# A block's outputs: the centre's share added by TensorE in layer one, maximum and moments spread over two blocks in layer two

## The chip, the cores and the metric

The kernel runs on one core of a Trainium2 chip. The core has five engines with a queue of instructions each: TensorE (PE in the profile, with its weight loads as PEld), VectorE (DVE), ScalarE (ACT), GpSimd (POOL) and SyncE (SP), which here only issues DMA transfers. SBUF is the working memory with 128 partitions. PSUM is the memory that TensorE writes its results to, in banks of 512 float32 values per partition. The metric is device time in microseconds (us); lower is better.

## The reference

The model is one block of three parts, each added to `x` (16 batches, 32 channels, 512 positions): a graph attention over neighbours, a state-space scan, and a small feed-forward part. The change touches the first one only. Its inputs are coordinates of 512 nodes in each of 16 batches. Four space-filling curves (Morton and Hilbert, each with two axis orders) give four orders of the nodes. Then, twice (layer one and layer two):

```python
neigh = gather(feats, inds)                  # k = 10 neighbours of a node along a curve, for 4 curves
gf = concatenate([broadcast(center), neigh - center], axis=-1)
x16 = stack(...)[..., perm].reshape(B*N, k, total).astype(float16)   # total = 2 * C * 4 = 256
scores = einsum('bihd,bjhd->bhij', qh, qh) / sqrt(32)                # 8 heads of 32, 10 x 10 each
out = einsum('bhij,bjhd->bihd', softmax(scores), qh)
fused = out @ W_lin.T + b_lin                                        # 64 values per node and neighbour
h = einsum('oc,bnkc->bonk', W_conv, fused)                           # 32 channels in layer one, 64 in two
h = lrelu(instance_norm(h, (2, 3)))          # mean and variance over nodes and neighbours
feats_next = h.max(axis=-1)                  # greatest over the 10 neighbours
```

Normalisation and leaky ReLU are increasing functions, so the greatest value over the neighbours may be taken before them. From each block of `h` two things are then needed: the greatest of every 10 values, and the running moments (count, mean, spread) of all values.

## The kernel before

A chunk of four batches fills the 128 partitions (4 batches x 32 channels), so there are four chunks. A chunk in a layer is a stage; `order` lists the eight stages as (chunk, layer) with layers counted from 0: (0,0), (1,0), (0,1), (1,1), (2,0), (3,0), (2,1), (3,1). The text numbers them 1 to 8. Stages 1, 2, 5, 6 are layer one and stages 3, 4, 7, 8 layer two. A stage has 43 blocks of 12 nodes (the last has 8), so there are 344 blocks.

The loop at L993 is a software pipeline written out by hand: round `it` does a different step of several blocks, and every engine executes its instructions in the order in which the round writes them.

- `scores` (L812, TensorE) multiplies the neighbour differences `DD` with themselves into the bank `s`; `greatest` (L821, DVE) takes the maximum over each row of `s` with its sign turned, `c`; a round later `expo` adds `c` to `s` by TensorE (L829) and ACT takes the exponential (L834).
- `sums` (L841) and `shares` (L847 on DVE, L849 on POOL) normalise it; `turn` (L855, DVE) transposes it two rounds later.
- `mapped` (L874, TensorE, 48 matmuls, copied by ACT at L879) multiplies the differences with the folded weights. `outputs` (L893, TensorE, lag 3) multiplies attention and mapped values into the bank `h`.
- `reduce` (lag 4) takes `h` when it is full. The bank `h` holds four blocks of layer one (one tile of 480 values per partition) or two blocks of layer two (two tiles of 240). There is one such bank (`bufs=1`). DVE adds the centre's share `hc` to it and writes the sum to SBUF (L908, `hs`), then takes the maxima from `hs` (L912) and the moments (L914, one instruction for each tile).
- `hc` is that part of `h` which comes from the centre and the bias alone: one value per node and channel, the same for its 10 neighbours. It is made once per stage, by a matmul at L655 and ACT at L656.
- Beside this, `steps` does a piece of the next stage's preparation (`prep`: casts, 0/1 matrices `oh` at L723 on DVE, their matmuls at L689) or of the last stage's end (`end`, normalisation). `rank_step` compares sorting keys (L538 on TensorE, L539 on ACT), twice a round at first, then once, until 256 comparisons are done.

DVE's order in a round is thus: `turn`, `reduce` (one round in four in layer one, in two in layer two), `greatest`, `sums`, `steps`, `shares`. TensorE's is: `expo`, `scores`, comparison, `mapped`, `steps`, comparison, `outputs`. SP carries the transfers of `DX` (the differences rearranged), of the keys, and of the preparation; POOL has `shares` and the differences (L770).

Of the kernel before, what the change touches and what calls it, by code (L numbers as in the profile page):

```python
# [8 lines left out]
F32 = mybir.dt.float32  # L9
# [4 lines left out]
ALU = mybir.AluOpType  # L14
AX = mybir.AxisListType
# [3 lines left out]
P = 128  # L19
B = 16  # L20
C = 32
D = 512
NBG = 4
M = 4
K = 10
NG = 12
NGRP = -(-D // NG)
NB = 3
QB = NB * K
# [23 lines left out]
def kernel(ctx: ExitStack, tc: tile.TileContext, I, out):  # L53
# [64 lines left out]
    with ExitStack() as cx:  # L118
        graph_part(nc, tc, cx, I, dram, id32, ones, xt, U, layernorm_steps, rstd_steps, scan_input)
# [256 lines left out]
def graph_part(nc, tc, cx, I, dram, id32, ones, xt, F0, layernorm_steps, rstd_steps, scan_input):  # L376
# [10 lines left out]
    start = ExitStack()  # L387
# [14 lines left out]
    for L, co in ((1, 32), (2, 64)):  # L402
        for n, shape in (("wlA", [64, P]), ("wlC", [64, P]), ("wcT", [64, co]), ("bl", [64, 1])):
            t = wp.tile(shape, F32, name=f"{n}{L}")
            nc.sync.dma_start(out=t, in_=I[f"{n}{L}"])
            loaded[n, L] = t
    for dst, v, at in ((own, -1.0, (0, 4)), (others, 1.0, (2, 7))):
        t = kp.tile([M * B, D], BF16, name=f"sign{at[0]}")
# [12 lines left out]
    layers = []  # L421
# [127 lines left out]
    def rank_step(tile_of):  # L549

        n = ranked[0]
        if n == 4 * M * B:
            return
        ranked[0] += 1
        if n < FIRST:
            half, k = divmod(n, HALF)
            b, c, m = half % 4, k // 2, 2 * (half // 4) + k % 2
        else:
            b, k = divmod(n, 4 * M)
            c, m = divmod(k, M)  # L560
        if n == 0:
            load_keys(0, (0, 1))
        compare(tile_of(n), b, c, m)
        if n < FIRST:
            if k == 1 and half != 3 and half < 7:
                load_keys((half + 1) % 4, (0, 1) if half < 3 else (2, 3))
        elif k == 4 and b + 1 < B:
            load_keys(b + 1, range(M))
# [39 lines left out]
    sm = cx.enter_context(tc.tile_pool(name="gsm", bufs=3))  # L608
# [174 lines left out]
    live = {}  # L783
    state = {}

    def begin(at):
        g, layer = order[at]
        L, co, npair, WA, WC, HB = layers[layer]
        key = keys[at]
        per = 4 // npair  # L790
        nst = -(-NGRP // per)
        mxo = wk.tile([P, npair, D], F32, tag="mxo", name=f"mxo{key}")
        stats = wk.tile([P, npair, nst, 6], F32, tag="stats", name=f"stats{key}")
        state[at] = key, co, npair, WA, made[key][2], per, mxo, stats
# [87 lines left out]
    def outputs(at, gi):  # L882
        key, co, npair, WA, hc, per = state[at][:6]
        us, e = live.pop(("us", at, gi)), live.pop(("e2", at, gi))
        slot = gi % per
        if slot == 0:
            live["h", at] = ps_1.tile([P, npair, per * NQ], F32, tag="h", name=f"h{at}_{gi}")
        h = live["h", at]
        for j in range(NJ):
            for b in range(4):  # L890
                pr, r = divmod(b * co, P)
                q0 = slot * NQ + j * QB
                nc.tensor.matmul(  # L893
                    h[r:r + co, pr, q0:q0 + QB], lhsT=us[:, j, b * co:(b + 1) * co],
                    rhs=e[:, 4 * j + b, :QB], start=True, stop=True,
                )
        if slot == per - 1 or gi == NGRP - 1:
            live["full", at, gi] = h

    def reduce(at, gi):  # L900
        key, co, npair, WA, hc, per, mxo, stats = state[at]
        h = live.pop(("full", at, gi), None)
        if h is None:
            return
        f0 = (gi - gi % per) * NG
        nn = min((gi + 1) * NG, D) - f0
        hs = sm.tile([P, npair, per * NG, K], F32, tag="hs", name=f"hs{at}_{gi}", bufs=1)
        nc.vector.tensor_tensor(  # L908
            hs[:, :, :nn], h[:, :, :nn * K].rearrange("p r (n j) -> p r n j", j=K),
            hc[:, :, f0:f0 + nn].unsqueeze(3).to_broadcast([P, npair, nn, K]), ALU.add,  # L910
        )
        nc.vector.tensor_reduce(mxo[:, :, f0:f0 + nn], hs[:, :, :nn], AX.X, ALU.max)  # L912
        for pr in range(npair):
            nc.vector.bn_stats(stats[:, pr, gi // per], hs[:, pr, :nn].rearrange("p n j -> p (n j)"))  # L914
        if gi == NGRP - 1:
            tails.append(end(at))

    def end(at):

        g, layer = order[at]  # L920
        key, co, npair, WA, hc, per, mxo, stats = state.pop(at)
        res = []
        for pr in range(npair):
            mv = sm.tile([P, 2], F32, tag="mv", name=f"mv{key}_{pr}")
            nc.vector.bn_aggr(mv, stats[:, pr].rearrange("p k s -> p (k s)"))
            r = sm.tile([P, 1], F32, tag="hr", name=f"hr{key}_{pr}")
            yield from rstd_steps(sm, r, mv[:, 1:2], 1, f"h{key}_{pr}")
            dst = F1[g] if layer == 0 else wk.tile([P, D], F32, tag=f"F2_{pr}", name=f"F2_{key}_{pr}", bufs=1)
            yield from lrelu_norm(dst, mxo[:, pr], mv[:, 0:1], r, f"{key}_{pr}")
            res.append(dst)  # L930
        if layer == 1:
            yield from finish(g, res)

    def lrelu_norm(dst, src, mean, r, key):
        t = wk.tile([P, D], F32, tag="lr", name=f"lr{key}", bufs=1)
        nc.vector.tensor_scalar(t, src, mean, r, ALU.subtract, ALU.mult)
        yield
        nc.vector.scalar_tensor_tensor(dst, t, 0.2, t, ALU.mult, ALU.max)
        yield

    def junk(q):
        return wk.tile([P, D], F32, tag="h3", name=f"usq{q}", bufs=1)

    def finish(g, F2):
        p3 = ps_1.tile([P, D], F32, tag="misc", bufs=2, name=f"p3_{g}")
        for j, f in enumerate((F0[:, g], F1[g], *F2)):
            nc.tensor.matmul(p3, lhsT=W3[:, j], rhs=f, start=(j == 0), stop=(j == 3))
        h3 = wk.tile([P, D], F32, tag="h3", name=f"h3_{g}", bufs=1)
        nc.scalar.copy(h3, p3)
        yield  # L950
        n3 = wk.tile([P, D], F32, tag="n3", name=f"n3_{g}", bufs=1)
        yield from layernorm_steps(sm, n3, h3, f"f{g}")
        yield
        nc.vector.scalar_tensor_tensor(n3, n3, 0.2, n3, ALU.mult, ALU.max)
        nc.vector.tensor_tensor(xt[:, g], xt[:, g], n3, ALU.add)

    made = {}
    order = [(0, 0), (1, 0), (0, 1), (1, 1), (2, 0), (3, 0), (2, 1), (3, 1)]
# [13 lines left out]
    def steps(at, gi):  # L972


        if tails:
            if next(tails[0], tails) is tails:
                tails.pop(0)
            return
        if at + 1 >= len(order):
            return  # L980
        if at + 1 not in ahead:
            if at > 0 and gi < 4:
                return
            ahead[at + 1] = [prep(*order[at + 1]), PREP]
        a = ahead[at + 1]
        for _ in range(2 if a[1] > NGRP - LEAD - 1 - gi else 1):
            if next(a[0], None) is False:
                break
            a[1] -= 1

    ahead = {}
    blocks = [(at, gi) for at in range(len(order)) for gi in range(NGRP)]
    for it in range(len(blocks) + 4):  # L993

        def do(step, lag):
            if 0 <= it - lag < len(blocks):
                step(*blocks[it - lag])

        at, gi = blocks[it] if it < len(blocks) else (len(order), 0)
        if gi == 0 and it < len(blocks):  # L1000
            begin(at)
        do(expo, 1)
        do(turn, 3)
        do(scores, 0)
        do(reduce, 4)
        rank_step(later_tile)
        do(greatest, 0)
        do(mapped, 0)
        do(sums, 1)
        if at + 1 == len(order) and gi == 4:  # L1010
            tails.extend(scan_input(sm, junk(q), q) for q in range(NBG - 1))
        steps(at, gi)
        do(shares, 1)
        if ranked[0] < 8 * 4 * M:
            rank_step(later_tile)
        do(outputs, 3)
        if it + LEAD < len(blocks):
            to, g2 = blocks[it + LEAD]
            if g2 == 0:
                for _ in ahead[to][0]:  # L1020
                    pass
            differences(to, g2)
# [384 lines left out]
```

## Time and profile before

| | |
|---|---|
| median of 3 runs | 2433.89 us (2430.68 to 2434.2) |
| profiled execution | 2429.63 us, span from first to last instruction 2427.9 us |
| TensorE busy | 2137.0 us, 88% of the span; weight loads 1249.5 us |
| DVE busy | 1739.6 us, 72% |
| ACT busy | 1099.8 us, 45% |
| POOL busy | 831.7 us, 34% |
| granted TensorE clock | 0.969 of full, mean |
| L908 (addition) | 132 instructions, 81.8 us, 620 ns each |
| L912 (maxima) | 132 instructions, 84.2 us, 638 ns each |
| L914 (moments) | 220 instructions, 89.1 us, 438 ns each |

Busy time is the union of an engine's instructions. TensorE's ends are modelled and some of its records can be missing, so its idle time is to be read with care. In the waits, "A <- B: total, times, longest" says that A's engine stood idle until B ended. In the groups, the time after the second bar is idle time of the engine just before them. In a timeline, columns are start, length (both in us), engine, line, operation, and in brackets idle time before it and what ended it. An instruction's start on DVE may come a little before the one before it ends, so prices of a queue are read from start to start.

### The profile page before, as it was taken

The numbers are of one execution on the slowest core, as the hardware profiler recorded it, in microseconds if no ns is written. First come the engines' busy times: TensorE is split into PE (matmuls) and PEld (weight loads), VectorE is DVE, ScalarE is ACT, GpSimd is POOL, SyncE is SP. The second block draws the span as 40 slices with busy tenths as digits, with TensorE's granted clock in tenths as the row PEclk, the third lists the DMA queues.
The fourth block names the chain that finished last, engine by engine and source line by source line (L and its number), as shares of the span: only waits on it lengthen the run. The fifth ranks groups of instructions, "written<-read, shape, count | busy, mean of one in ns | idle before, by whom it ended". The sixth has DMA issues, their size and how long they took to land. (4 is left out here: it accounts for less than half of the span.)

```text
span 2427.9 us, 88565 instructions
## 1 busy us (share of the span) xinstructions
PE 2137.0 (88%) x39024; PEld 1249.5 (51%) x39146; DVE 1739.6 (72%) x3718; ACT 1099.8 (45%) x2023; POOL 831.7 (34%) x897
## 2 busy tenths in 40 slices
PE   5598687999898777789999789999999999999979
PEld 2254455677666455557767544444444444444422
DVE  8498798888898899989999866553553626446643
ACT  6686556667554334345555323333332423333331
POOL 2165556445445465664645300020211202021200
PEclk9899899999999989999999889999999999999989
DMA  1323232231132231422311312203112131210000
GB/s 48 79 54 76 49 77 59 50 72 40 36 71 51 51 83 42 95 49 55 68 38 35 96 48 73 76 26 100 52 57 67 38 87 40 81 54 22 27 36 18
DMA packets 121625, 137.99 MB, mean 57 GB/s; under 512 B 18398, under 2 KB 79506, under 8 KB 121154
## 3 DMA queue, kind: packets, MB, share of 16 engines
q1 hardware_dynamic: 121240, 132.32, 22.1%
q8 instruction: 307, 5.03, 0.9%
q14 instruction: 78, 0.64, 0.1%
HBM read 77.02 MB, written 12.85 MB: 37 GB/s over the span
## 5 line engine op out<-in xcount | busy, mean ns | idle before, releaser
L849 POOL TENSOR_TENSOR EN<-e,rz 128x480 f32<-128x480 f32 x344 | 342.9, 997 | 562.7 <-DVE rz L847 417.8
L874 PE MATMUL u<-WA,DD 128*32 128x128 bf16 (+1 forms) x16512 | 421.9, 251 | 53.7 <-issue 36.7
L874 PEld LDWEIGHTS <-DD 128*32 128x32 f16 x16512 | 341.5, 99 | 71.8 <-issue 67.9
L879 ACT COPY us<-u 128x512 f32<-128x512 f32 x516 | 302.1, 587 | 152.5 <-PE u L874 134.2
L834 ACT ACTIVATE e<-s,smc 128x480 f32<-128x480 f32 x344 | 227.6, 662 | 293.6 <-PE s L829 266.0
L770 POOL TENSOR_TENSOR DD<-fs,crep 128x480 f16<-128x480 f32 (+2 forms) x344 | 350.2, 1019 | 0.0
L893 PE MATMUL h<-e,us 128*32 128x30 f32 (+1 forms) x11008 | 283.7, 211 | 57.4 <-DVE e L855 27.5
L893 PEld LDWEIGHTS h<-e,us 128*32 128x32 f32 (+1 forms) x11008 | 250.9, 127 | 145.0 <-issue 46.9
L1105 DVE SCALAR_TENSOR_TENSOR cyh<-ppch,t_conv_w,cyh 128x496 f32<-128x496 f32 (+2 forms) x192 | 137.4, 716 | 221.4 <-ACT cyh L1100 217.5
L821 DVE TENSOR_REDUCE c<-s 128x16 bf16<-128x480 f32 x344 | 218.9, 636 | 72.7 <-PE s L812 70.2
L1181 POOL TENSOR_TENSOR da<-lei,dA 128x512 f32<-128x512 f32 x32 | 40.6, 1271 | 612.5 <-PE pl L1186 577.9
L1254 PE MATMUL po<-wo,gs 128*128 128x512 f32 x512 | 240.5, 605 | 10.8 <-DVE xt L1257 10.6
L1093 PE MATMUL ppch<-hT,winch 128*128 128x512 f32 x512 | 232.2, 593 | 0.0
L1093 PE MATMUL ppg<-hT,wing 128*128 128x512 f32 x512 | 231.9, 593 | 0.0
L855 DVE STREAM_TRANSPOSE e<-EN 128x512 f32<-128x512 f32 x344 | 224.3, 652 | 0.6 <-POOL EN L849 0.6
L841 DVE TENSOR_REDUCE z<-e 128x16 f32<-128x480 f32 x344 | 219.0, 637 | 0.0
L539 ACT ACTIVATE sgn<-kd 128x512 bf16<-128x512 f32 x256 | 153.1, 598 | 56.8 <-PE kd L538 28.2
L723 DVE TENSOR_SCALAR oh<-it,rank 128x512 bf16<-128x512 f16 x512 | 168.7, 389 | 8.5 <-PE pp L689 8.5
L812 PEld LDWEIGHTS <-DD 128*32 128x32 f16 x5504 | 82.1, 97 | 164.1 <-issue 127.7
L829 PE MATMUL s<-c,idb 128*128 128x480 bf16 x344 | 131.6, 383 | 36.2 <-DVE c L821 33.4
L812 PE MATMUL s<-DX,DD 128*32 128x120 f16 x5504 | 144.0, 224 | 20.3 <-DMA DX<-DD 17.0
L1093 PEld LDWEIGHTS ppch<-hT,winch 128*128 128x128 f32 x512 | 93.7, 190 | 122.7 <-issue 122.3
(323 smaller groups left out, 2748.1 us busy)
## 6 DMA issues: line engine op xcount, KB each, us to landing
DX<-DD SPq DMA_DIRECT2D x456, 90.0 KB
wo<-in_out_proj SPq DMA_DIRECT2D x64, 256.0 KB
wing<-in_in_proj SPq DMA_DIRECT2D x64, 256.0 KB
winch<-in_in_proj SPq DMA_DIRECT2D x64, 256.0 KB
crep<-dC SPq DMA_DIRECT2D x128, 64.0 KB
dS<-so SPq DMA_DIRECT2D x32, 256.0 KB
fs<-dS SPq DMA_DIRECT2D x128, 64.0 KB
wincB<-in_in_proj SPq DMA_DIRECT2D x8, 256.0 KB
```

What stands on the lines that cost most here:

```text
L770: nc.gpsimd.tensor_tensor(d[:, :, m0 - n0:n1 - n0], win, crep[:, :, m0:n1].unsqueeze(3).to_broadcast([P, 4, n1 - m0, K]), ALU.subtract,)
L812: nc.tensor.matmul(s[rh, j * 4 * QB:(j + 1) * 4 * QB].rearrange("p (b q) -> p b q", b=4), lhsT=d[:, h, c0:c0 + 32], rhs=dx[:, h, :, c0:c0 ...
L821: nc.vector.tensor_reduce(c, live["s", at, gi].rearrange("p (i q) -> p i q", q=QB), AX.X, ALU.max, negate=True)
L834: nc.scalar.activation(e, s.rearrange("p (i q) -> p i q", q=QB), AF.Exp, scale=smc)
L841: nc.vector.tensor_reduce(z, e, AX.X, ALU.add)
L849: nc.gpsimd.tensor_tensor(en[:, :, :QB], e, rz.unsqueeze(2).to_broadcast([P, NI, QB]), ALU.mult)
L855: nc.vector.transpose(e.rearrange("p i q -> p (i q)"), en.rearrange("p i q -> p (i q)"))
L874: nc.tensor.matmul(u[rh, jj], lhsT=d[:, h, c0:c0 + 32], rhs=WA[k][:, h].rearrange("p b o -> p (b o)"), start=(jj == 0 and k == 0), stop=(k ...
L879: nc.scalar.copy(us[:, j - jj:j + 1], u)
L893: nc.tensor.matmul(h[r:r + co, pr, q0:q0 + QB], lhsT=us[:, j, b * co:(b + 1) * co], rhs=e[:, 4 * j + b, :QB], start=True, stop=True,)
L1093: nc.tensor.matmul(pp, lhsT=w[:, k], rhs=hT[:, k], start=(k == 0), stop=(k == 3))
L1254: nc.tensor.matmul(po, lhsT=gs[:, i, q * P:(q + 1) * P], rhs=wo[i], start=(i == 0), stop=(i == TG - 1))
```

## The change

In layer one (`npair == 1`), the first `outputs` of a group now begins with one more matmul: the identity `id32` times `hc`, each value repeated 10 times, put into all used columns of the bank `h`. The 64 matmuls (16 in each of four blocks) of the group's `outputs` that follow add to it (`start=False`), where they overwrote before. DVE's addition L908 is gone in layer one; maxima and moments read the bank `h` itself, so the bank is in use until both have read it.

In layer two the addition stays. In the round of the addition only the moments of the first tile are taken. The maxima and the moments of the second tile are kept as a function in `live["rest", at]`, and are executed in the next round by the new step `rest`, ahead of `reduce`; after the last group of a stage at once. The loop has one more round.

```diff
         if slot == 0:
             live["h", at] = ps_1.tile([P, npair, per * NQ], F32, tag="h", name=f"h{at}_{gi}")
+            if npair == 1:
+
+                f0 = gi * NG
+                nn = min(f0 + per * NG, D) - f0
+                nc.tensor.matmul(
+                    live["h", at][:, 0, :nn * K].rearrange("p (n j) -> p n j", j=K), lhsT=id32,
+                    rhs=hc[:, 0, f0:f0 + nn].unsqueeze(2).to_broadcast([P, nn, K]), start=True, stop=False,
+                    skip_group_check=True,
+                )
...
-                    rhs=e[:, 4 * j + b, :QB], start=True, stop=True,
+                    rhs=e[:, 4 * j + b, :QB], start=npair > 1, stop=True, skip_group_check=True,
...
-        hs = sm.tile([P, npair, per * NG, K], F32, tag="hs", name=f"hs{at}_{gi}", bufs=1)
-        nc.vector.tensor_tensor(
-            hs[:, :, :nn], h[:, :, :nn * K].rearrange("p r (n j) -> p r n j", j=K),
-            hc[:, :, f0:f0 + nn].unsqueeze(3).to_broadcast([P, npair, nn, K]), ALU.add,
-        )
-        nc.vector.tensor_reduce(mxo[:, :, f0:f0 + nn], hs[:, :, :nn], AX.X, ALU.max)
-        for pr in range(npair):
-            nc.vector.bn_stats(stats[:, pr, gi // per], hs[:, pr, :nn].rearrange("p n j -> p (n j)"))
+        hs = h[:, :, :nn * K].rearrange("p r (n j) -> p r n j", j=K)
+        if layers[order[at][1]][0] == 2:
+            t = sm.tile([P, npair, per * NG, K], F32, tag="hs", name=f"hs{at}_{gi}", bufs=1)
+            nc.vector.tensor_tensor(
+                t[:, :, :nn], hs, hc[:, :, f0:f0 + nn].unsqueeze(3).to_broadcast([P, npair, nn, K]), ALU.add,
+            )
+            hs = t[:, :, :nn]
+
+        def greatest_of():
+            nc.vector.tensor_reduce(mxo[:, :, f0:f0 + nn], hs, AX.X, ALU.max)
+
+        def moments(pr):
+            nc.vector.bn_stats(stats[:, pr, gi // per], hs[:, pr].rearrange("p n j -> p (n j)"))
+
+        if npair == 1:
+            greatest_of()
+            moments(0)
+        else:
+            moments(0)
+            live["rest", at] = lambda: (greatest_of(), moments(1))
         if gi == NGRP - 1:
+            rest(at, gi)
             tails.append(end(at))
+
+    def rest(at, gi):
+        if ("rest", at) in live:
+            live.pop(("rest", at))()
...
-    for it in range(len(blocks) + 4):
+    for it in range(len(blocks) + 5):
...
+        do(rest, 5)
         do(reduce, 4)
```

## The prediction

> **What bounds the kernel now.** I read the busy time by stretches first. The graph part runs from 117 to about 1376 us as eight stages of 43 blocks; the stretches below are cut at the first exponential of each stage. Stages 1, 2, 5, 6 are layer one, stages 3, 4, 7, 8 layer two (columns: length; busy time of PE, weight loads, DVE, ACT, POOL; granted clock; DMA).
>
> ```profile
> 117.00:267.00 150.00, 123.83 (x4409) 72.86 (x4418) 122.85 (x271) 104.11 (x242) 84.32 (x93) 0.95 0.29 62
> 267.00:414.00 147.00, 112.31 (x4422) 75.47 (x4461) 129.78 (x288) 88.34 (x183) 86.24 (x95) 0.95 0.30 65
> 414.00:585.00 171.00, 158.35 (x4419) 118.96 (x4457) 146.58 (x337) 113.11 (x224) 86.57 (x96) 1.00 0.25 56
> 585.00:763.00 178.00, 164.60 (x4424) 122.48 (x4450) 153.79 (x365) 104.56 (x203) 86.23 (x95) 0.96 0.24 52
> 763.00:915.00 152.00, 114.70 (x4422) 77.00 (x4421) 138.96 (x319) 58.71 (x101) 86.16 (x96) 0.92 0.29 62
> 915.00:1056.00 141.00, 107.20 (x4415) 72.90 (x4414) 129.24 (x284) 58.97 (x97) 86.28 (x95) 0.96 0.30 65
> ```
>
> Layer two is TensorE's: 158 of 171 us and 165 of 178 us, and most of its blocks come at even steps of 3.21, 3.65 or 4.29 us with TensorE idle 0 to 0.25 us in each. Layer one differs by stage. In stages 5 and 6 DVE is busy 91 to 92% and TensorE 75 to 76%; in stage 1 the two are level (82%). There the two engines take turns at the lead, so neither total alone tells what an edit is worth. Next I read who waits for the exponent's constant, `c`: one line of the waits in each layer-one stretch, in order of time.
>
> ```profile
> PE s L829 <- DVE c L821: 1.8, 4, 0.6
> PE s L829 <- DVE c L821: 5.6, 8, 1.4
> PE s L829 <- DVE c L821: 11.5, 10, 1.4
> PE s L829 <- DVE c L821: 7.6, 10, 1.4
> ```
>
> In stages 2, 5 and 6 TensorE waits for `c` in 28 blocks, nearly always the one in four whose DVE work has the three `reduce` steps ahead of `greatest`. Stage 1 hardly has this wait: with two rank comparisons per block TensorE arrives later than `c`. The timeline of one reduce block in stage 5 shows the wait, and one in stage 1 its absence:
>
> ```profile
> 859.47 0.61 DVE L908 TENSOR_TENSOR hs<-h,hc 128x480 f32<-128x480 f32 x1
> ...
> 860.13 0.46 PE L893 MATMUL h<-e,us 128*32 128x30 f32 x32 [0.47 <-DVE hs L908]
> ...
> 861.94 0.36 PE L829 MATMUL s<-c,idb 128*128 128x480 bf16 x1 [1.35 <-DVE c L821]
> ```
>
> ```profile
> 137.93 0.46 PE L893 MATMUL h<-e,us 128*32 128x30 f32 x32
> ...
> 138.44 0.36 PE L829 MATMUL s<-c,idb 128*128 128x480 bf16 x1
> ```
>
> The groups give the prices (line, engine, shape, count | busy, mean ns | idle before):
>
> ```profile
> L908 DVE TENSOR_TENSOR hs<-h,hc 128x480 f32<-128x480 f32 x124 | 78.7, 635 | 31.3 <-PE h L893 31.2
> L912 DVE TENSOR_REDUCE mxo<-hs 128x48 f32<-128x480 f32 x124 | 81.0, 653 | 4.3
> L914 DVE BATCH_NORM_STATS2 stats<-hs 128x6 f32<-128x480 f32 x40 | 26.0, 650 | 0.0
> L821 DVE TENSOR_REDUCE c<-s 128x16 bf16<-128x480 f32 x344 | 218.9, 636 | 72.7 <-PE s L812 70.2
> L841 DVE TENSOR_REDUCE z<-e 128x16 f32<-128x480 f32 x344 | 219.0, 637 | 0.0
> L655 PE MATMUL ph<-c,WC 128*128 128x512 f32 x24 | 16.4, 769 | 15.3 <-DVE c L650 14.5 <-ACT us L879 0.7
> ```
>
> **Removed: the layer-one addition.** Four stages have 11 groups each (ten of 48 nodes and one of 32), so 44 of the 132 additions go. In the block above L908 starts at 859.47 and L912 at 860.11, 0.64 us apart, so DVE gets 44 x 0.64 = 28 us back, if DVE is what the block waits for.
>
> **Added: one seed matmul per layer-one group.** No such instruction is in the trace; the nearest row is L655, also f32 with a full 128x128 weight. Each is two records; in the timeline the work behind it starts 1.06 or 1.07 us after it in 7 of 12 cases, with the first weight load exposed, and once 0.93 us; projections of L1093, with loads hidden, follow each other at 0.43 us per record. For 480 of 512 columns that is 0.80 us (loads hidden) to 1.0 us. I take 0.9 us, nearer the first, since the identity waits for nothing and can be loaded ahead: 44 x 0.9 = 40 us of TensorE. The seed adds no DMA and nothing on POOL or ACT.
>
> **The seed waits longer for the bank.** There is one `h` bank. It was free after L908; now it is free after the maximum and the moments, 0.6 us later. Behind the waiting seed stand the group's `outputs`, the next block's L829 and its scores, and ACT's exponential waits for those. [...] The row decides otherwise: after the block above, bank free at 860.75 (859.47 + 0.58 + 0.65 + 0.05), seed to 861.65, outputs 0.4, next L829 at 862.05. Before it stood at 861.94, held by `c`. `c` is now ready at 861.25. So the wait for `c` is exchanged for the seed, at +0.1 us on TensorE and -0.64 us on DVE.
>
> **Reading the bank twice.** [...] The trace has the same reduction from both memories, L821 from the bank and L841 from SBUF: 636 and 637 ns. [...]
>
> **What the layer-one stages make of it**, group by group, from the idle time of both engines:
> - Stage 1: in 8 of 11 groups TensorE is idle 0 to 1.0 us in 12 to 13 us (one, 2.8), and DVE mostly 0.8 to 2.2. The seed lies in the open: 8 x 0.9 = 7.2, less what idle time swallows, +5.5 (ends +2, +8). Its stall of 14.5 us for the transfer into `fs` (at 236 us) stays as it is.
> - Stage 2: one comparison per block is left. Five groups have DVE full (idle under 0.2) and TensorE with 2.2 to 2.8 us idle, some of which are lost matmul records; they gain about 0.2 each. The others lose about 0.2: in the block at 304 us the next L829 goes from 307.0 to 307.5. Sum 0 (-2, +4).
> - Stages 5 and 6: twelve groups with DVE full gain. Not the whole 0.64: after the block above, scores would be ready at 866.9 and DVE at 866.8, so 0.45 on average, 12 x 0.45 = 5.4; ten groups lose 0.1. Sum -4.4 (-8, +2).
>
> **Layer two: one order exchanged for another.** The 88 additions stay; the maximum and one moment move to the next block, ahead of its `greatest`. DVE's sum over two blocks stays. In the block with the addition, `c` comes 0.57 + 0.32 = 0.9 us earlier; in the next DVE starts 0.9 us earlier and does 0.9 us more first, so `c` comes when it did, or into slack of 1.0 us or more. What can be won is TensorE's wait for `c` there: 0, 0.7, 1.5 and 5.1 us in the four stages, 7.3 us. But in stages 7 and 8, where it lies, DVE is idle only 0.1 to 0.5 us per four blocks: it is full, and the wait would return elsewhere. At the change of stages the chain of casts to L655 stands behind a reduce (TensorE waits 2.7 and 3.6 us) and could win 0.9 each. I take -2.5 (-5, 0). The bank is freed by the addition as before, the moved steps issue nothing on SP or POOL and pass no wait of another engine, and the last group of a stage is finished at once as before; the loop's one extra round has nothing else to do.
>
> **Sum.** +5.5 + 0 - 4.4 - 2.5 = -1.4 us. The profiled execution took 2429.63 us (span 2427.9 and 1.7 around it); it becomes 2428.2. The median of the runs is 2433.89, 4.3 above it; against that, **2432.5 us**.
>
> **Rivals.** *DVE leads nearly everywhere (faster).* For it: DVE's 88 to 92% in stages 2, 5, 6. Nineteen DVE-full groups at the whole 0.64 are -12, layer two's waits in part -4, stage 1 only +3: -13, 2421 us. Against: DVE idles 12 to 28 us in each of these stages.
> *TensorE leads after the seed (slower).* 44 x 0.9 = 40 us of seeds, of which the waits for `c` in layer one cover 26.5, and nothing of DVE's gain is seen: +13, 2447 us. It decides once TensorE has under 0.9 us of true idle time per group; stage 1 has that. Against: 1.9 to 4.7 us are idle in the full-DVE groups of stages 5 and 6.
> *The gains and losses cancel:* my forecast. There the change does what it says in each stage, and the total does not show it.
>
> **How the numbers follow.** About 0.2% (4.9 us) is what a measurement of this kernel can tell from no change. My case 0.5, faster rival 0.27, slower rival 0.23. My case by itself spans 2426 to 2439, so it gives 0.06 to faster and 0.02 to slower: faster 0.33, same 0.42, slower 0.25. Adding all good ends gives -13, all bad ends +14; the range reaches to about two thirds of either, 2424 to 2442.
>
> **What would show it.** L908's successor has 88 entries; layer-one maximum and moments near 640 to 660 ns from the bank; 88 seed records at 0.8 to 1.0 us per pair. The first stage 2 to 8 us longer, stages 5 and 6 shorter by 1 to 4 each, TensorE's wait for `c` in layer one nearly gone, replaced by waits of the seed for the moments. I am wrong if the seed takes over 1.2 us, if reading the bank costs DVE 60 ns or more, if stages 5 and 6 do not shorten, or if layer two moves by more than 5 us.

## The result, and the profile after

The changed kernel takes 2415.49 us (median of 6 runs, 2411.28 to 2418.40) against 2433.89 us: a ratio of 0.9924 with a 95% interval of 0.9911 to 0.9937, so 18.4 us faster. The forecast was 2432.5 us with a range of 2424 to 2442; the result lies below it, and most of the miss is in layer two. Measured twice more, beside other kernels, the ratio was 0.9928 and 0.9933.

The profiled execution took 2416.21 us (span 2414.5). Busy time by stretches, stages 1 to 6, in the columns of the prediction (length; PE, weight loads, DVE, ACT, POOL; granted clock; DMA):

```profile
114.00:268.00 154.00, 137.11 (x4445) 76.11 (x4444) 117.45 (x263) 104.97 (x242) 85.57 (x95) 0.94 0.29 62
268.00:412.00 144.00, 127.72 (x4447) 74.98 (x4445) 121.85 (x274) 88.50 (x182) 86.39 (x96) 0.99 0.30 66
412.00:586.00 174.00, 171.71 (x4490) 120.65 (x4489) 143.52 (x333) 113.12 (x224) 85.82 (x95) 0.98 0.25 55
586.00:757.00 171.00, 167.62 (x4456) 119.86 (x4452) 151.74 (x365) 104.60 (x203) 85.61 (x95) 0.99 0.25 55
757.00:910.00 153.00, 120.82 (x4449) 76.72 (x4446) 132.71 (x310) 58.82 (x101) 86.22 (x95) 0.93 0.28 60
910.00:1052.00 142.00, 113.23 (x4438) 72.20 (x4436) 122.70 (x275) 58.89 (x96) 87.22 (x97) 0.98 0.30 65
```

In layer one DVE has 5.4 to 7.9 us less to do per stage. In layer two (third and fourth line) it should have exactly what it had, since no instruction was removed; yet it is busy 143.52 instead of 146.58 us and 151.74 instead of 153.79. That is the first sign of the cause. The groups by shape (count | busy, mean ns | idle before):

```profile
L919 DVE TENSOR_TENSOR hs<-h,hc 128x480 f32<-128x480 f32 x84 | 54.0, 642 | 27.3 <-PE h L902 27.3
L925 DVE TENSOR_REDUCE mxo<-hs 128x48 f32<-128x480 f32 x84 | 51.0, 607 | 0.0
L892 PE MATMUL h<-hc,id 128*128 128x480 f32 x80 | 42.7, 617 | 13.8 <-DVE stats L928 12.8 <-DVE hs L919 0.9
L925 DVE TENSOR_REDUCE mxo<-h 128x48 f32<-128x480 f32 x40 | 25.1, 626 | 4.1 <-PE h L902 4.0
L928 DVE BATCH_NORM_STATS2 stats<-h 128x6 f32<-128x480 f32 x40 | 25.9, 648 | 0.0
L829 PE MATMUL s<-c,idb 128*128 128x480 bf16 x344 | 132.4, 385 | 5.5 <-DVE rz L847 3.2 <-DVE c L821 1.3
```

The seed (L892) is two records; from its start to the outputs behind it 0.90 to 1.00 us pass in 38 of the 40 full groups, median 0.97. Maxima and moments read from the bank cost 626 and 648 ns, no more than the 653 and 650 ns from SBUF in the kernel before. TensorE's wait for `c` (last row) is 1.3 us in all. In the kernel before it was 33.4 us:

```profile
L829 PE MATMUL s<-c,idb 128*128 128x480 bf16 x344 | 131.6, 383 | 36.2 <-DVE c L821 33.4
```

The seed now waits 12.8 us for the moments. By window, in stages 2, 5 and 6:

```profile
PE h L892 <- DVE stats L928: 2.5, 3, 1.3
PE h L892 <- DVE stats L928: 7.4, 6, 1.9
PE h L892 <- DVE stats L928: 2.8, 4, 1.0
```

### The profile page after: what moved, and what is told of

It is laid out like the page before. It is cut to its first block, busy times and chain, and to the rows that moved or that the text cites. A ratio compares the mean times of both kernels' runs of the same rounds, so it can differ in the third digit from the quotient of the medians.

```text
span 2414.5 us, 88867 instructions
## 1 busy us (share of the span) xinstructions
PE 2190.0 (91%) x39234; PEld 1248.1 (52%) x39234; DVE 1699.6 (70%) x3674; ACT 1100.1 (46%) x2023; POOL 831.6 (34%) x897
## 5 line engine op out<-in xcount | busy, mean ns | idle before, releaser
L879 ACT COPY us<-u 128x512 f32<-128x512 f32 x516 | 302.0, 587 | 149.5 <-PE u L874 131.8
L821 DVE TENSOR_REDUCE c<-s 128x16 bf16<-128x480 f32 x344 | 220.7, 642 | 107.0 <-PE s L812 104.4
L855 DVE STREAM_TRANSPOSE e<-EN 128x512 f32<-128x512 f32 x344 | 224.4, 652 | 0.0
L841 DVE TENSOR_REDUCE z<-e 128x16 f32<-128x480 f32 x344 | 219.5, 638 | 0.0
L723 DVE TENSOR_SCALAR oh<-it,rank 128x512 bf16<-128x512 f16 x512 | 158.0, 368 | 7.5 <-PE pp L689 7.5
L1120 PEld LDWEIGHTS ppg<-hT,wing 128*128 128x128 f32 x512 | 95.8, 190 | 114.0 <-issue 114.0
```

The lines of the kernel that those rows point to most:

```text
L821: nc.vector.tensor_reduce(c, live["s", at, gi].rearrange("p (i q) -> p i q", q=QB), AX.X, ALU.max, negate=True)
L841: nc.vector.tensor_reduce(z, e, AX.X, ALU.add)
L855: nc.vector.transpose(e.rearrange("p i q -> p (i q)"), en.rearrange("p i q -> p (i q)"))
L879: nc.scalar.copy(us[:, j - jj:j + 1], u)
L1120: nc.tensor.matmul(pp, lhsT=w[:, k], rhs=hT[:, k], start=(k == 0), stop=(k == 3))
```

## The experiments

Unless said otherwise an edit is to the kernel before, and the figure is the median against the kernel before measured beside it, with the ratio's interval. From here on "comparison" means an instruction of L723, by which VectorE makes a 0/1 matrix `oh`, and not the comparison of keys on TensorE (L538). "Held" counts those of L723 that take over 500 ns; the kernel before has 48 in layer one and 13 in layer two.

### Each layer alone

One kernel has layer one as changed and layer two as before, the other the reverse:

```
# l1_only: layer two keeps its order       # l2_only: no seed, addition in both layers
 else:                                      if False:                     # the seed
+    greatest_of()                          ...
+    moments(0)                             if True:                      # the addition
+    moments(1)                             (the split of layer two as changed)
```

> Layer one as in the changed kernel (seed by TensorE, no addition on DVE), layer two as before. The theory read from the two traces: layer one's four stages change by +1 to +3 us in all (seed in the open in stage 1, gain in the others), so the ratio is 0.999 to 1.002. The rival that DVE leads layer one nearly everywhere: -8 to -14 us, ratio 0.994 to 0.997. The rival that the seed leads: +8 us or more, ratio over 1.003.

> Layer one as before, layer two as in the changed kernel (maxima and second moments a round later). The theory read from the two traces: layer two carries the gain, -10 to -16 us, ratio 0.993 to 0.996, and TensorE's wait for c in the layer-two stages falls from 7 us to under 2. The forecast's own sum for layer two: -2.5 us, ratio 0.998 to 1.000.

> Layer one as changed, layer two as before, once more, beside layer two alone. If the two parts share a gain, or the first measurement was high, this run and the next one come to 17 to 20 us together; if they add up only to 26 us again, the two parts share some 8 us when both are there. This one alone: -10.5 us again if its first value stands, -4 to -7 us if it was high.

> Layer two as changed, layer one as before, once more, beside layer one alone. -15.4 us again if its first value stands; -11 to -13 us if it was high.

Layer one alone: 2425.74 against 2436.26 us (0.9956, 0.9942 to 0.9969), and again 2428.56 against 2433.30 (0.9971, 0.9957 to 0.9986): 7 to 10.5 us faster. Layer two alone: 2420.84 against 2436.26 (0.9935, 0.9922 to 0.9948), and again 2420.54 against 2433.30 (0.9944, 0.9926 to 0.9963): 13 to 15.4 us faster. So both parts gain, layer two more. By the mean ratios the parts would make 23 us together, and the whole kernel gains 16 to 18; what the two have in common in these 5 to 6 us was not found, and with intervals of some 3 us on each part it may in part be measurement.

### The addition and the seed by themselves

`l1_nocentre` drops the addition in layer one and adds no seed; it leaves the centre's share out there. `l1_seedcost` keeps the addition and seeds the bank with zeros:

```
# l1_nocentre                               # l1_seedcost
-if npair == 1:   # seed                    -rhs=hc[:, 0, f0:f0 + nn]...
+if False:                                  +rhs=nil...     # zeros
 if layer is two:  # addition               -if layer is two:  # addition
                                            +if True:
```

> Layer one without the addition on DVE and without the seed, so the centre's share is left out of layer one's values; maxima and moments read the bank; layer two as before. It shows what DVE's 28 us are worth when TensorE pays nothing. My group count (DVE full in 19 groups, 0.64 us each, and nothing elsewhere): -8 to -13 us, ratio 0.9945 to 0.997. If DVE leads everywhere: -20 to -28 us. If TensorE leads and the longer hold of the bank hurts: 0 to -4 us.

> Layer one keeps VectorE's addition as before and TensorE puts a product of zeros into the bank as well, so the 44 seed matmuls (40 us of TensorE by the forecast's 0.9 us each) come on top and nothing is taken away; layer two is as before. By the forecast the seed lies in the open in the eight groups of stage 1 and in half of it elsewhere: +5.5 us in stage 1 and +8 to +14 us in all. By the difference of the runs with and without the seed (2425.74 less 2423.55) it costs about +2 us: 0 to +4. More than +8 says that the forecast priced the seed rightly and only VectorE's part wrongly.

Without the additions: 2423.55 us (0.9951, 0.9938 to 0.9964), 12 to 13 us of the 28 that VectorE no longer works. With the seed on top and nothing taken away: 2431.72 against 2432.01 us (1.0008, 0.9996 to 1.0019), some 2 us at most 5. So the forecast's share in the open was too large. Where the forty microseconds of matmuls went is less plain: TensorE's idle time took them, or in part its clock paid for them, for the mean granted clock of these executions is 0.970 against 0.964 beside it. No run separates the two.

### Earlier greatest values without the spreading

`l2_late` issues layer two's maxima and second moments in the same round, but behind `greatest`:

```
 do(reduce, 4)
 do(greatest, 0)
+do(rest, 4)
```

> Layer one as before. In layer two the maxima and the second tile's moments stay in the same round, but stand behind greatest on DVE's queue instead of ahead of it. If the gain of layer two comes only from c being ready earlier for TensorE, this gives the same as the split over two rounds, -10 to -16 us. If it comes from spreading DVE's work over two rounds, at most half of it, 0 to -6 us, because sums, the 0/1 matrices and shares of that round come as late as before.

2431.24 against 2436.26 us (0.9986, 0.9977 to 0.9996): 3 to 5 us of layer two's 13 to 15. So the earlier `c` is worth a quarter to a third, and something in spreading the work over two rounds is worth the rest.

### What the spreading removes

The trace shows it. A round without a reduction in stage 7 of the kernel before, VectorE and then GpSimd (start, duration, engine, line, operation):

```profile
1141.92 0.65 DVE L855 STREAM_TRANSPOSE e<-EN 128x512 f32<-128x512 f32 x1
1142.50 0.62 DVE L821 TENSOR_REDUCE c<-s 128x16 bf16<-128x480 f32 x1
1143.05 0.63 DVE L841 TENSOR_REDUCE z<-e 128x16 f32<-128x480 f32 x1
1143.60 1.50 DVE L723 TENSOR_SCALAR oh<-it,rank 128x512 bf16<-128x512 f16 x4
...
1142.17 1.00 POOL L849 TENSOR_TENSOR EN<-e,rz 128x480 f32<-128x480 f32 x1 [2.77 <-DVE rz L847]
1143.13 1.03 POOL L770 TENSOR_TENSOR DD<-fs,crep 128x480 f16<-128x480 f32 x1
```

Four comparisons take 1.50 us. In the round with a reduction ahead of this one they take 1.13 us, from 1140.72. Here the first of them started while GpSimd subtracts (`DD`, 1143.13 to 1144.16) and takes 0.71 us; it ends 0.15 us after the subtraction does. The same kind of round in the changed kernel:

```profile
1132.91 0.65 DVE L855 STREAM_TRANSPOSE e<-EN 128x512 f32<-128x512 f32 x1
1133.49 0.60 DVE L925 TENSOR_REDUCE mxo<-hs 128x48 f32<-128x480 f32 x1
1134.02 0.39 DVE L928 BATCH_NORM_STATS2 stats<-hs 128x6 f32<-128x240 f32 x1
1134.33 0.64 DVE L821 TENSOR_REDUCE c<-s 128x16 bf16<-128x480 f32 x1
1134.89 0.64 DVE L841 TENSOR_REDUCE z<-e 128x16 f32<-128x480 f32 x1
1135.45 1.13 DVE L723 TENSOR_SCALAR oh<-it,rank 128x512 bf16<-128x512 f16 x4
...
1134.12 1.04 POOL L770 TENSOR_TENSOR DD<-fs,crep 128x480 f16<-128x480 f32 x1
```

The deferred maxima and moments now stand ahead, the subtraction runs beside moments and reductions, which take no longer for it (0.39 and 0.64 us here; by their rows 0.40 and 0.64), and the comparisons begin after it: four in 1.13 us. GpSimd starts its two operations when `rz` is there, so they end 2.4 us after `rz` starts; `rz`, the transposition, `c` and `z` fill only 1.84 us of VectorE, and the deferred 0.84 us bridge the gap. In stage 7 the comparisons' row goes from

```profile
L723 DVE TENSOR_SCALAR oh<-it,rank 128x512 bf16<-128x512 f16 x64 | 22.1, 402 | 0.0
```

to

```profile
L723 DVE TENSOR_SCALAR oh<-it,rank 128x512 bf16<-128x512 f16 x64 | 18.4, 346 | 0.0
```

3.7 us, and the stage, from its first exponential to the next stage's, from 159.9 to 155.9 us. Stage 8 has no comparisons, but small instructions met the subtraction there. In the kernel before:

```profile
1268.03 0.58 DVE L76 TENSOR_TENSOR rsh_s<-rsr_s 128x1 f32<-128x1 f32 x1
1268.64 0.16 DVE L77 TENSOR_TENSOR rsh_s<-rsh_s,rst_s 128x1 f32<-128x1 f32 x1
...
1267.56 1.03 POOL L770 TENSOR_TENSOR DD<-fs,crep 128x480 f16<-128x480 f32 x1
```

In the changed kernel:

```profile
1259.11 0.15 DVE L76 TENSOR_TENSOR rsh_s<-rsr_s 128x1 f32<-128x1 f32 x1
1259.29 0.16 DVE L77 TENSOR_TENSOR rsh_s<-rsh_s,rst_s 128x1 f32<-128x1 f32 x1
```

An instruction on one column takes 0.58 us instead of 0.15. In layer two of the kernel before, 13 comparisons lose 4.8 us in this way and some ten other instructions (L76, L641, L938, L954) 4.3 us, some 9 us together; in the changed kernel one of them is left (an L76, 0.4 us). With the 3 to 5 us of the earlier `c` that is 12 to 14 us of layer two's 13 to 15; the sum is near, and each part has some 2 to 3 us of doubt.

One rival is the granted clock, which also differs between the kernels (see the last section). It can be set aside where a stage has the same clock in both: stage 7 takes 159.9 us before and 155.9 to 156.2 us in three profiles of the changed kernel, all at 0.98; stage 8 takes 151.7 and, in the profile with full clock, 148.4 us, both at 1.00. So these two stages gain 3 to 4 us each without it.

Not every instruction of VectorE that starts while GpSimd works is held. In the rounds above L723 is (0.71 us) and L76 is (0.58 us); L821, which starts inside the subtraction at 1134.33, is not (0.64 us). Over the whole trace of the kernel before, 65 comparisons start while an instruction of GpSimd has over 0.25 us to go, with a median of 709 ns against 345 for those beside none; 31 transpositions (L855) that start so take 653 ns, like the others, and 41 moments of 240 columns (L914) 400 ns against 395. What in the hardware sets the one kind apart from the other, no run here shows.

### Taking the subtraction away

GpSimd's subtraction is cut to the first node of each block outside stage 1; the other nodes' differences are left out. The same with layer one, and with layer two, as changed:

```
 m0 = max(first, half)
+if at > 0 and first > 0:
+    n1 = m0 + 1
```

> The kernel before, with GpSimd's subtraction of each block (1.03 us) cut to its first node from the third stage's blocks on and in the second stage's as well, except in a tile's first block; the other nodes' differences are left out, and nothing else is changed. VectorE's one-hot comparisons (L723) that start while that subtraction runs take 0.7 us instead of 0.34, 54 of them in stages 2 to 7, 20.3 us in all beyond 0.345 us each. If VectorE is held there by GpSimd, these long ones go to nearly none, and the time falls: by the 5.5 us of stages 3, 4 and 7 if layer one has the room to hide its part, by 10 to 14 us if layer one's part counts at the rate that its additions counted (12.7 us for 28). If the long ones have another cause, they stay and the time moves by less than 2 us.

> Layer one as changed, layer two as before, and GpSimd's subtraction cut to one node as in the run of the kernel before with the short subtraction (-27.3 us; the other nodes' differences are left out). If layer one gains by VectorE's additions alone, it gains as much on top of that run as on top of the kernel before: -34 to -39 us against the kernel before. If part of its gain is that its comparisons meet GpSimd less often (17.3 us before, 13.0 us with layer one changed), that part is gone: -31 to -34 us.

> Layer two as changed, layer one as before, and GpSimd's subtraction cut to one node (the other nodes' differences are left out). If layer two's gain is that its comparisons no longer meet GpSimd's subtraction (5.5 us of waiting before, 0.4 after, and some 1.5 us more in the other instructions that met it), at least 5 us of its 15 are already in the run with the short subtraction: -33 to -38 us. If the gain has nothing to do with GpSimd, all 15 us come on top of it: -40 to -44 us. If it is all GpSimd's, nothing comes on top: -26 to -30 us.

The kernel before with the short subtraction: 2404.76 against 2432.01 us (0.9884, 0.9868 to 0.9901), held comparisons 6 and 0. That is 27 us, at least twice what was expected, and near the waiting that is gone: 20 us of the comparisons and 4 us of the other instructions in layer two. On top of it the changes are worth nothing that can be measured. Layer two: 2404.36 against 2433.30 (0.9884, 0.9859 to 0.9909), as expected if its gain is all GpSimd's. Layer one: 2411.76 against 2433.30 (0.9906, 0.9888 to 0.9924). That is some 5 us slower than without the change, where 4 to 12 us faster had been expected; across two batches, with about 6 us of doubt, the slowdown is not shown, but the expected gain is not there. The run has the seed and the missing addition together, so it does not say which of them fails to pay.

These runs take most of a microsecond of GpSimd's work from each block besides the meeting, so they don't settle the cause alone, nor that all of the 27 us is VectorE's waiting.

### The meeting itself

Both kernels keep all work and add the same 54 instructions to VectorE, a reduction that nobody reads, in rounds in which the kernel before has a held comparison (54 of its 61). One puts it ahead of that comparison, the other behind:

```
+if count[0] in PADS:      # the held ones; or each of them + 1
+    nc.vector.tensor_reduce(pad1, id32[:, :118]...[P, 3, 118], AX.X, ALU.max)
+count[0] += 1
 nc.vector.tensor_scalar(oh, it2, rank..., None, ALU.is_equal)
```

> The kernel before with 54 more instructions on VectorE, each a reduction of 354 elements that nobody reads (about 0.43 us from its start to the next one's; 23 us in all), each directly ahead of one of the comparisons that take 0.7 us in the kernel before. If those comparisons are held until GpSimd's subtraction ends, the added instruction runs inside that time, the comparison behind it takes 0.34 us, and the time stays within 0 to +4 us. If they are slow for a reason of their own, the added work counts as VectorE's work does: +10 to +20 us.

> The same 54 instructions in the same rounds, but each one behind the comparison that is held and ahead of the next comparison. The comparison is held as before and the added work comes on top: +10 to +20 us at the rate of the additions in layer one (12.7 us for 28 us) up to nearly the whole of 23 us. If VectorE's time doesn't decide these rounds, or if the hold is of no account, it stands within 3 us of the run with the instructions ahead.

Ahead: 2430.18 against 2431.03 us (0.9994, 0.9982 to 1.0006). Behind: 2447.49 against 2431.03 (1.0070, 1.0052 to 1.0088). The same 23 us of added work cost nothing in the one place and 16 us in the other. The timeline of a round with the instruction ahead (held comparisons left: 4 and 0):

```profile
877.61 0.63 DVE L847 TENSOR_REDUCE z<-e 128x16 f32<-128x480 f32 x1
878.16 0.50 DVE L727 TENSOR_REDUCE pad<-id 128x3 f32<-128x354 f32 x1
878.59 1.13 DVE L729 TENSOR_SCALAR oh<-it,rank 128x512 bf16<-128x512 f16 x4
...
877.69 1.03 POOL L776 TENSOR_TENSOR DD<-fs,crep 128x480 f16<-128x480 f32 x1
```

and of the same round with it behind (48 and 15):

```profile
877.67 0.62 DVE L847 TENSOR_REDUCE z<-e 128x16 f32<-128x480 f32 x1
878.22 0.71 DVE L729 TENSOR_SCALAR oh<-it,rank 128x512 bf16<-128x512 f16 x1
878.85 0.51 DVE L727 TENSOR_REDUCE pad<-id 128x3 f32<-128x354 f32 x1
...
877.75 1.03 POOL L776 TENSOR_TENSOR DD<-fs,crep 128x480 f16<-128x480 f32 x1
```

The reduction that starts inside the subtraction runs at once (0.50 us); the comparison that starts there takes 0.71 us and ends 0.15 us after the subtraction does. So the meeting is what makes these comparisons long, and the time that VectorE loses by it counts: GpSimd's load is the same in both runs.

### Two ways around it, and the order once more

`after_ddsplit` issues the subtraction of the changed kernel as two halves. `split_both` has no seed and keeps VectorE's addition in layer one, but spreads it: addition, maxima, moments in three rounds.

```
# after_ddsplit                             # split_both, from l2_only
+mid = (m0 + n1) // 2                       if npair == 1:
+for ma, mb in ((m0, mid), (mid, n1)):      -    greatest_of(); moments(0)
     nc.gpsimd.tensor_tensor(...)           +    live["rest", at] = [greatest_of, lambda: moments(0)]
```

> The changed kernel once more, beside the other runs of this batch. If layer one alone (-10.5 us) and layer two alone (-15.4 us) add up, it stands 24 to 28 us under the kernel before. If the two get part of their gain from the same place, it stands 16 to 21 us under it, as in its own measurement (-18.4 us).

> The changed kernel with GpSimd's subtraction of a block issued as two of half the nodes, about 0.55 us each. If a comparison that VectorE starts during it is held until the instruction of GpSimd ends and not until the queue is empty, the 34 long comparisons that are left in layer one become shorter (12.2 us beyond 0.345 us each falls to 4 or less) and the time falls by 2 to 6 us against the changed kernel of this batch. If GpSimd's second half gets in ahead of the waiting comparison, they stay as long or longer, and the time is the same or up to 3 us more.

> Layer two as changed; layer one keeps VectorE's addition, has no seed, and spreads its reduction over three rounds: the addition in one, the maxima in the next, the moments in the third. VectorE has 28 us more to do than in the changed kernel, but three of four rounds in layer one, and not one of four, have 0.55 us of other work ahead of the comparisons. If the meeting with GpSimd decides, the long comparisons of layer one fall from 48 (32 in the changed kernel) to 16 or fewer, and the time is 2402 to 2412 us, below the changed kernel. If VectorE's total work decides, it is that of layer two alone or worse: 2418 to 2424 us.

> The changed kernel beside these two: 16 to 19 us under the kernel before, as in the two measurements before (ratios 0.9924 and 0.9928).

The halves: 2412.14 us beside 2414.43 for the changed kernel in the same batch (ratios to before 0.9915, 0.9900 to 0.9930, and 0.9928, 0.9914 to 0.9941), no difference; 41 comparisons are held in layer one, no fewer. In the trace all 41 start when the first half has ended (0 to 0.19 us before) and the second has begun, and each ends 0.15 us after the second half does. So they meet the second half alone, and the run does not show which would go first if a comparison stood waiting between the two.

`split_both`: 2409.12 us beside 2416.51 for the changed kernel (0.9906, 0.9892 to 0.9921, and 0.9933, 0.9920 to 0.9946). It is 7 us faster than the changed kernel though VectorE adds in both layers as before; its held comparisons are 13 in layer one (29 to 34 in the changed kernel) and none in layer two. It is the fastest complete version here.

`after_cfirst` was to defer layer two's maxima to the next round and put them behind `greatest` there:

```
-do(rest, 5)
 do(reduce, 4)
 do(greatest, 0)
+do(rest, 5)
```

> The changed kernel with the deferred maxima and second moments issued behind the next scores' greatest values instead of ahead of them; VectorE's work in each round is the same and the comparisons still stand behind it. If TensorE still waits for the greatest values in layer two, the time falls by 2 to 5 us against the changed kernel (2414 to 2416 us). If its wait for them is gone, as the trace of the changed kernel says (1.3 us in all), it stays within 2 us.

> The changed kernel with the maxima and second moments of layer two really deferred to the next round, and there issued behind the greatest values of the next scores. No comparison of layer two is held in either order, since the work ahead of the comparisons is the same. TensorE's wait for the greatest values is 1.3 us in all in layer two, so the time stays within 2 us of the changed kernel; if the earlier greatest values are worth something that the waits do not show, it falls by 3 to 5 us.

`after_cfirst` did not do so. Behind the reduction the call finds that round's own maxima and runs them at once, which makes it layer one as changed with `l2_late`, not what its expectation says. As that it fits: 2421.14 against 2431.03 us (0.9962, 0.9950 to 0.9975), 13 comparisons held in layer two again, and half of the changed kernel's gain gone. `after_cfirst2` remembers the block and defers in fact: 2423.80 us beside 2416.51 (0.9954, 0.9941 to 0.9966), none held in layer two, and still 7 us slower where 2 at most had been expected. Its profiled execution has a span of 2417.8 us against 2416.6, too near to find those 7 us in; they stay unexplained.

## Why the prediction was wrong

**Layer two, the step that failed.** "DVE's sum over two blocks stays", and then: in stages 7 and 8 "it is full, and the wait would return elsewhere": -2.5 us, at most -5. Measured: -13 to -15. DVE's instructions stayed the same; their durations did not. Part of what its row counts as busy was waiting for GpSimd, some 9 us in layer two, and the new order put other work into that time. The prediction shows what would have told this: its price rows hold a mean, and the comparisons of L723, which have a median of 345 ns and a maximum of 721 over the whole kernel, do not appear in it.

**Layer two, the chain of hand-offs and the earlier `c`.** Right in kind: TensorE's wait for `c` fell from 33.4 to 1.3 us in all. `l2_late` prices the earlier `c` at 3 to 5 us, where the forecast had -2.5 for all of layer two.

**Seed.** 0.9 us was near (0.97). What was wrong is where it lies: stage 1 was to be 5.5 us longer, and all 44 seeds on top of the old kernel cost about 2 us. From first exponential to first exponential, stage 1 takes 148.6 and 149.5 us in the two profiles of layer one alone and 152.7, 148.3 and 152.8 us in three of the changed kernel, against 149.5: no steady 5.5.

**The bank held longer.** Right: reading the bank costs nothing more (626 and 648 ns against 653 and 650), and the seed waits 12.8 us in all for the moments, where 0.6 us in each of the 44 groups would be 26 us.

**Layer one as a whole.** Forecast +1.1; measured -7 to -10.5. "28 us, if DVE is what the block waits for" was the right condition; 12.7 of the 28 came (`l1_nocentre`), not 5.4 on twelve groups. The step that failed is thus the count of groups in which VectorE leads. Why it leads in more of them than the idle times said is shown in part only: the held comparisons lose 17.2 us in layer one before and 12.6 and 11.8 us in the two profiles of layer one alone, and with the subtraction short the gain is gone. The rest stays open.

**The rivals.** "DVE leads nearly everywhere", at 2421 us, had the right sign and came nearest, but its layer two (-4) was sized by the same step. What was held against it, that DVE idles 12 to 28 us in each of these stages, reads the rows too high: in stages 2, 5 and 6 the length less the busy time is 17, 13 and 12 us, and 27 belongs to stage 1.

## What to carry to other kernels

Before calling an engine full, ask its rows for the spread of a duration, not the mean: an instruction whose maximum is twice its median may be waiting inside its own busy time, and a change of order elsewhere can then win that back. In this kernel the ones to look at were VectorE's instructions that start inside GpSimd's subtraction: the comparisons L723 (a median of 709 ns against 345), the cast L641 (850 against 426) and the one-column L76 (580 against 150), but not the reductions L841 (643 against 642). A reduction put in front of the comparisons cost nothing (2430.18 against 2431.03 us). Moving work to another engine paid here less than spreading the same work over rounds (`split_both` is 7 us ahead of the changed kernel).

## What the runs showed that had not been expected

A VectorE instruction on one column takes 580 ns instead of 150 when it starts inside GpSimd's subtraction. Twenty-three microseconds of extra work on an engine that is up to 92% busy cost nothing where they fill such a wait.

Profiles differ by whole steps of TensorE's clock (3.4 or 6.8 us of a stage at half of it), beside any edit. Stage 3 takes 170.6 to 171.4 us in the profiles in which its clock is full throughout (seven, among them the kernel before, layer one alone and two of the changed kernel) and 173.6 to 174.5 us in the twelve in which it is halved for 6.8 us, whatever the edit, and 172.0 us in the one with 3.4 us: about half of the halved time is the difference. In the first profile of the changed kernel it was halved (granted 0.98, 174 us), and in that of the kernel before it wasn't (1.00, 171 us). So a single profile's stage length doesn't tell an edit of 3 us unless the clock is the same.

The medians take many executions, but the clock differs between kernels in them too. Its mean over the executions is 0.964 to 0.965 for the kernel before, 0.972 for the changed kernel in each of its three measurements, 0.970 for layer one alone, 0.966 and 0.968 for layer two alone. As an estimate from these figures, the halved clock takes 86 us of 2432 before and 68 us of 2415 after, a difference as large as the whole gain. It isn't the gain by itself: with the seed on top (0.970) and with the instruction ahead of the comparison (0.966) the clock rises and the time stays, and the short subtraction gains most at 0.969. But whether layer one's part, and what stages 7 and 8 leave of layer two's, came through the clock was not separated.
